# Layer 3's attention: sums of normalized tokens with channels on partitions, Wv applied after the sums

## The chip, the cores and the metric

One core of a Trainium2 chip runs the whole program: four layers over one image of 256 channels and 64 x 64 positions, that is 4096 tokens of 256 channels, all in fp32. The metric is the device time of one execution in microseconds. The engines are TensorE (PE, with its weight loads shown apart as PEld), VectorE (DVE), ScalarE (ACT), GpSimd (POOL) and SyncE (SP, which here issues transfers). Each works through its own queue in order and waits for others by semaphores.

## The reference, cut to the attention of layer 3

The layer norm of the tokens enters a plain attention of one head with 256 channels. Everything around it (two convolution-like layers, another attention, two mixtures of experts) is not touched.

```python
def _ln_t(v, eps=1e-5):
    m = jnp.mean(v, axis=-1, keepdims=True)
    s = jnp.var(v, axis=-1, keepdims=True)
    return (v - m) / jnp.sqrt(s + eps)

def _L3_attn_ref(x, Wq, bq, Wk, bk, Wv, bv):
    Q = jnp.einsum('bsd,de->bse', x, Wq) + bq
    K = jnp.einsum('bsd,de->bse', x, Wk) + bk
    V = jnp.einsum('bsd,de->bse', x, Wv) + bv
    scale = 1.0 / jnp.sqrt(jnp.asarray(Q.shape[-1], dtype=jnp.float32))
    scores = jnp.einsum('bqd,bkd->bqk', Q, K) * scale
    weights = jax.nn.softmax(scores, axis=-1)
    return jnp.einsum('bqk,bkd->bqd', weights, V)

t = t + _L3_attn_ref(_ln_t(t), Wq, bq, Wk, bk, Wv, bv)
t = t + _L3_ffn_ref(_ln_t(t), ...)
```

Since the weights of a query sum to 1, the bias bv can be added to the tokens once, and Wv can be applied before or after the weighted sum over keys: sum(w n) Wv = sum(w (n Wv)).

## The kernel before

The tokens `t` stay in SBUF as 32 tiles of 128 tokens (NT = 32), grouped in 8 blocks of 4 tiles (NBLK, TPB; NB = 512 tokens). Constants: P = 128, C = 256.

The work around the change is `attn3`. It runs in these stages.

1. *The expert layer of layer 2* (`experts`, L1879) writes its rows to `ys` in device memory.
2. *Preparation* (L1884 to L1895), over 8 blocks of 4 tiles. `combine` loads two rows per token from `ys` (one transfer through SP's queue, one through ACT's) and adds both to `t` (L1820, VectorE). `layer_norm` takes mean and variance (L195, L196), the root on ACT (L199), and writes `n` by ACT (L206). `to_channels` transposes it into `nT`, which has channels on partitions (TensorE L217, copies out of PSUM by ACT L220 and VectorE L222). Then Wv is applied to every tile, two tiles to a PSUM bank (L1894, two accumulating matmuls per tile), and ACT copies the result into `v` (L1895), which has 257 columns per tile: the last is 1.0, so that the same matmul that sums the values also sums the exponentials.
3. *The attention loop* (L1925 to L1964), over nine blocks of queries: seven of 4 tiles and two of 2 (`sizes`). For each block it steps over all 32 tiles of keys. A step has `scores(j)`: two matmuls of the key tile with the block's queries into one bank of `s` (three buffers), and an exponential on ACT into `e` (four buffers, L1940). And `values(j)`: for each of the block's query tiles one matmul with a 128x128 piece of `e` as the loaded weights and `v[:, j, :]` streamed past, into that tile's own accumulator `o{i}` (L1945). The scores of step j+1 stand ahead of the values of step j on TensorE. At the end of a block VectorE takes the reciprocal of column 257 and updates the tokens (L1958, L1959).
4. *Between the steps* stand the next block's queries (`queries`, L1916 to L1918, at the step j = 28) and, in portions at j = 3, 7, 11, and so on, the router of the block before (`route`, L1587 to L1645): layer norm, transposes, router matmul, the choice of two experts by small operations of VectorE, and eight indirect transfers issued by POOL. Their PSUM tiles come from `bank()`. PSUM has 8 banks: four for `o`, three for `s`, one (`q`) for queries and router. In the two half blocks two of the `o` banks are lent to `bank()`.
5. After the last block its router portion runs alone, then `tile_table`, then layer 3's expert layer.

Additions that do not depend on the attention also stand in this code: `t += bv3` per block (L1931) and a reduction of `nT` for a guard value (L1933). The order on each queue is settled when the kernel is compiled, by a scheduler that may move independent instructions past each other; on the compiled queue of VectorE the additions and reductions just named stand in the preparation.

Of the kernel before, what the change touches and what calls it, by code (L numbers as in the profile page):

```python
# [10 lines left out]
F32 = mybir.dt.float32  # L11
# [3 lines left out]
ALU = mybir.AluOpType  # L15
# [4 lines left out]
P = 128  # L20
C = 256
HW = 64
N = HW * HW
NT = N // P
NB = 512
NBLK = N // NB
TPB = NB // P
# [51 lines left out]
def bc(ap, axis, n):  # L79

    ap = ap.unsqueeze(axis)
    shape = list(ap.shape)
    shape[axis] = n
    return ap.to_broadcast(shape)


class Net:
# [1766 lines left out]
    def attn3(self, t, S):  # L1854

        nc, tc, w = self.nc, self.tc, self.w

        sizes = [TPB] * (NBLK - 1) + [TPB // 2] * 2  # L1860
        with tc.tile_pool(name="a3", bufs=1) as pool:
            nT = pool.tile([P, 2, N], F32, tag="nT", name="a3_nT")
            v = pool.tile([P, NT, C + 1], F32, tag="v", name="a3_v")
            nc.gpsimd.memset(v[:, :, C : C + 1], 1.0)

            big = pool.tile([P, 2, 2, len(sizes)], F32, tag="big", name="a3_big")
            nc.gpsimd.memset(big, 0.0)
            wqk = pool.tile([P, 2, C], F32, tag="wqk", name="a3_wqk")
            bqk = pool.tile([P, 2], F32, tag="bqk", name="a3_bqk")
            with tc.tile_pool(name="a3m_ps", bufs=1, space=PSUM) as ps:  # L1870
                wT = w["w_qkT3"]
                for m in range(2):
                    p = ps.tile([P, C], F32, tag=f"w{m}", name="a3_w_ps")
                    self.mm(p, [(wT[:, kt, m * P : (m + 1) * P], wT[:, kt, C:]) for kt in range(2)])
                    nc.vector.tensor_copy(wqk[:, m, :], p)
                    p = ps.tile([P, 1], F32, tag=f"b{m}", name="a3_b_ps")
                    self.mm(p, [(wT[:, kt, C + m * P : C + (m + 1) * P], self.par("bq3", kt)) for kt in range(2)])
                    nc.vector.tensor_copy(bqk[:, m : m + 1], p)
            self.experts(S)  # L1879
            with (  # L1880
                tc.tile_pool(name="a3n", bufs=2) as wp,
                tc.tile_pool(name="a3n_ps", bufs=2, space=PSUM) as ps,
            ):
                for b in range(NBLK):  # L1884
                    tiles = slice(b * TPB, (b + 1) * TPB)
                    self.combine(b, t, wp)
                    n = wp.tile([P, TPB, C], F32, tag="n", name="a3_n")
                    self.layer_norm(wp, t[:, tiles, :], n, 1e-5, on_act=True)
                    self.to_channels(ps, "tr", n, nT[:, :, b * NB : (b + 1) * NB])
                    for i in range(0, TPB, 2):  # L1890
                        p = ps.tile([P, 2, C], F32, tag="v", name="a3_v_ps")
                        for j in range(2):
                            at = (b * TPB + i + j) * P
                            self.mm(p[:, j], [(nT[:, kt, at : at + P], w["w_v3"][:, kt, :]) for kt in range(2)])  # L1894
                        nc.scalar.copy(v[:, b * TPB + i : b * TPB + i + 2, :C], p)  # L1895
            with (
                tc.tile_pool(name="a3w", bufs=2) as wp,
                tc.tile_pool(name="a3_ps", bufs=1, space=PSUM) as ps,
            ):
                banks = ["q"]  # L1900

                def bank():
                    banks.append(banks.pop(0))
                    return ps.tile([P, NB], F32, tag=banks[-1], name="a3_q_ps")

                def route(t0, T):
                    rn = wp.tile([P, TPB, CX], F32, tag="rn", name="f_n")
                    rT = wp.tile([P, 2, NB], F32, tag="rT", name="f_nT")
                    return self.route(t0, T, t, S, wp, rn[:, :T], rT[:, :, : T * P], bank)

                def queries(b, t0):
                    T = sizes[b]
                    qT = wp.tile([P, 2, NB], F32, tag="qT", name="a3_qT")[:, :, : T * P]
                    for m in range(2):
                        p = bank()[:, : T * P]
                        self.mm(p, [(wqk[:, kt, m * P : (m + 1) * P], nT[:, kt, t0 * P : (t0 + T) * P]) for kt in range(2)])  # L1916
                        nc.scalar.activation(qT[:, m, :], p, AF.Identity, bias=bqk[:, m : m + 1])
                    nc.vector.tensor_reduce(big[:, 0, :, b : b + 1], qT, AX.X, ALU.max, apply_absolute_value=True)  # L1918
                    return qT

                steps = iter(())
                S["L"] = 3
                qT = queries(0, 0)
                t0 = 0
                for b, T in enumerate(sizes):  # L1925
                    o = [ps.tile([P, NB], F32, tag=f"o{i}", name="a3_o_ps") for i in range(T)]
                    if T < TPB:
                        banks[:] = ["q", "o2", "o3"]

                    part = t[:, t0 : t0 + T, :]  # L1930
                    nc.vector.tensor_tensor(part, part, bc(self.row("bv3"), 1, T), ALU.add)  # L1931
                    if b < NBLK:
                        nc.vector.tensor_reduce(big[:, 1, :, b : b + 1], nT[:, :, b * NB : (b + 1) * NB], AX.X, ALU.max,  # L1933
                                                apply_absolute_value=True)

                    def scores(j):
                        p = ps.tile([P, NB], F32, tag="s", name="a3_s_ps", bufs=3)[:, : T * P]
                        self.mm(p, [(nT[:, m, j * P : (j + 1) * P], qT[:, m, :]) for m in range(2)])
                        e = wp.tile([P, NB], F32, tag="e", name="a3_e", bufs=4)[:, : T * P]
                        nc.scalar.activation(e, p, AF.Exp, scale=1.0 / 16.0)  # L1940
                        return e

                    def values(j, e):
                        for i in range(T):
                            nc.tensor.matmul(o[i][:, : C + 1], e[:, i * P : (i + 1) * P], v[:, j, :], start=(j == 0), stop=(j == NT - 1))  # L1945

                    e = scores(0)
                    for j in range(NT):
                        nxt = scores(j + 1) if j + 1 < NT else None
                        values(j, e)  # L1950
                        e = nxt
                        if j % 4 == 3:
                            next(steps, None)
                        if j == NT - 4 and b + 1 < len(sizes):
                            qT_next = queries(b + 1, t0 + T)
                    for i in range(T):
                        r = wp.tile([P, 1], F32, tag="r", name="a3_r", bufs=4)
                        nc.vector.reciprocal(r, o[i][:, C : C + 1])  # L1958
                        nc.vector.scalar_tensor_tensor(t[:, t0 + i, :], o[i][:, :C], r, t[:, t0 + i, :], ALU.mult, ALU.add)  # L1959
                    qT = qT_next  # L1960
                    for _ in steps:
                        pass
                    steps = route(t0, T)
                    t0 += T  # L1964
                for _ in steps:
                    pass
                self.tile_table(S, wp, bank)

                top = wp.tile([P, 2, 2], F32, tag="top", name="a3_top")
                nc.vector.tensor_reduce(top, big, AX.X, ALU.max)  # L1970
                nc.vector.tensor_tensor(top[:, 0], top[:, 0], top[:, 1], ALU.mult)
                nc.vector.tensor_reduce(self.flags[:, 2:3], top[:, 0], AX.X, ALU.add)
# [235 lines left out]
```

## Time and profile before

| what | us |
|---|---|
| three runs: median (lowest to highest) | 4101.22 (4100.05 to 4104.15) |
| the profiled execution: time, span | 4099.97, 4098.3 |
| preparation: first combine addition to first query matmul | 2502.96 to 2561.22 |
| attention loop: first score matmul to last token update | 2565.86 to 3499.73 |
| one full block of the loop, from one query reduction (L1918) to the next | 2673.21 to 2790.34: 117.13 |
| layer 3's experts: from the first expert transpose (L1743) | 3521.04 |

All times inside the program are counted from the start of the span. Over the span TensorE is busy 87%, VectorE 42%, ACT 31%, GpSimd 35%. These are averages over stages with different limits; what a change in one stage is worth has to be read in that stage. The end of a matmul in the profile is modelled and groups overlap by some 0.2 to 0.4 us, so that distances between starts are to be used, not lengths. An fp32 matmul shows as two rows, each with its own weight load.

### The profile page before, as it was taken

The numbers are of one execution on the slowest core, as the hardware profiler recorded it, in microseconds if no ns is written. First come the engines' busy times: TensorE is split into PE (matmuls) and PEld (weight loads), VectorE is DVE, ScalarE is ACT, GpSimd is POOL, SyncE is SP. The second block draws the span as 40 slices with busy tenths as digits, with TensorE's granted clock in tenths as the row PEclk, the third lists the DMA queues.
The fourth block names the chain that finished last, engine by engine and source line by source line (L and its number), as shares of the span: only waits on it lengthen the run. The fifth ranks groups of instructions, "written<-read, shape, count | busy, mean of one in ns | idle before, by whom it ended". The sixth has DMA issues, their size and how long they took to land.

```text
span 4098.3 us, 57080 instructions
## 1 busy us (share of the span) xinstructions
PE 3563.3 (87%) x21872; PEld 2338.6 (57%) x21872; DVE 1738.9 (42%) x4404; ACT 1267.3 (31%) x2588; POOL 1445.4 (35%) x1376
## 2 busy tenths in 40 slices
PE   7879999999977767656678797999999999799997
PEld 4423433333335656544456575666666668688886
DVE  6876656565653554556566557011011101211111
ACT  4424343434423535311112234122222212233331
POOL 1258898888952243433334341000000001111110
PEclk9989999999998978878778798999999999899999
DMA  1003414210023111110001484000000000455554
GB/s 52 2 26 109 126 57 136 58 39 33 26 94 109 51 44 49 44 30 0 1 11 43 137 259 145 0 10 1 11 11 11 11 11 14 167 193 192 191 190 174
DMA packets 137792, 294.09 MB, mean 72 GB/s; under 512 B 14817, under 2 KB 72802, under 8 KB 128290
## 3 DMA queue, kind: packets, MB, share of 16 engines
q1 hardware_dynamic: 113138, 234.80, 17.7%
q0 software_dynamic: 13056, 35.93, 2.3%
q10 hardware_dynamic: 11312, 19.55, 1.4%
q8 instruction: 178, 2.92, 0.3%
q14 instruction: 108, 0.88, 0.1%
HBM read 202.53 MB, written 87.70 MB: 71 GB/s over the span
## 4 chain that ended last, share of the span: by engine, by line
PE 35%; issue 11%; DVE 5%; POOL 3%; DMA 2%; ACT 1%; SPq 0%; ACTq 0%; POOLq 0%; DVEq 0%
PE a_o_ps L1945 11%; PE a_s_ps L144 11%; PE f_h_ps L144 2%; PE a_qkv_ps L144 2%; PE f_y_ps L144 2%; POOL ys L1782 2%; DMA ys<-f_y,f_at 1%; PE a_q_ps L144 1%; DVE a_sm L1309 1%; PE tr_ps L217 1%; DMA f_g<-ys 1%; PE a_o_ps L144 1%; PE a_u_ps L144 1%; PE a_c_ps L1334 1%; POOL a_tmp L1165 0%
## 5 line engine op out<-in xcount | busy, mean ns | idle before, releaser
L565 POOL TENSOR_TENSOR l_sm<-l_sc,mask 128x512 f32<-128x512 f32 (+3 forms) x624 | 769.9, 1268 | 119.5 <-ACT l_sc L555 117.4
L559 DVE TENSOR_TENSOR l_sm<-l_s,mask 128x256 f32<-128x256 f32 (+3 forms) x1248 | 492.2, 447 | 302.7 <-PE l_s L549 292.9
L555 ACT COPY l_sc<-l_s 128x384 f32<-128x384 f32 (+3 forms) x896 | 367.5, 461 | 558.9 <-PE l_s L549 537.1
L1945 PE MATMUL a_o_ps<-a_v,a_e 128*128 128x257 f32 x2048 | 489.2, 380 | 0.0
L144 PE MATMUL a_s_ps<-a_qT,a_nT 128*128 128x512 f32 (+1 forms) x1152 | 487.8, 546 | 0.0
L1945 PEld LDWEIGHTS a_o_ps<-a_v,a_e 128*128 128x128 f32 x2048 | 388.9, 190 | 147.0 <-issue 103.8
L549 PE MATMUL l_s<-l_q,l_k 32*128 32x384 f32 (+2 forms) x3584 | 423.8, 514 | 7.1 <-ACT l_sc L555 4.1
L1641 POOL DMA_INDIRECT xs<-f_n,f_to x64 | 62.4, 975 | 883.6 <-DVE f_to L1638 840.9
L1940 ACT ACTIVATE a_e<-a_s_ps 128x512 f32<-128x512 f32 (+1 forms) x288 | 158.0, 549 | 687.3 <-PE a_s_ps L144 687.2
L144 PE MATMUL f_h_ps<-f_xT,f_w 128*128 128x256 f32 x1440 | 344.1, 387 | 15.2 <-ACT f_h L1755 5.5
L1782 POOL DMA_INDIRECT ys<-f_y,f_at x144 | 139.6, 970 | 571.3 <-ACT f_y L1781 545.4
L144 PE MATMUL f_y_ps<-f_w,f_h 128*128 128x256 f32 x1440 | 328.1, 379 | 0.0
L144 PEld LDWEIGHTS f_h_ps<-f_xT,f_w 128*128 128x128 f32 x1440 | 264.8, 191 | 83.7 <-ACT f_h L1755 31.5
L854 PE MATMUL l_acc_ps<-ident,l_pr 128*128 128x128 f32 x1600 | 208.9, 291 | 117.8 <-DVE l_pr L850 114.1
L549 PEld LDWEIGHTS l_s<-l_q,l_k 32*128 32x128 f32 x3584 | 164.6, 183 | 240.6 <-issue 123.2
L144 PEld LDWEIGHTS a_s_ps<-a_qT,a_nT 128*128 128x128 f32 x1152 | 216.3, 190 | 129.9 <-issue 112.9
L144 PEld LDWEIGHTS f_y_ps<-f_w,f_h 128*128 128x128 f32 x1440 | 268.2, 190 | 33.7
L854 PEld LDWEIGHTS l_acc_ps<-ident,l_pr 128*128 128x128 f32 x1600 | 193.8, 151 | 132.7 <-DVE l_pr L850 126.4
L850 DVE TENSOR_TENSOR l_pr<-l_vk,l_w_ps 128x1280 f32<-128x1280 f32 x128 | 182.1, 1480 | 91.0 <-ACT l_w_ps L839 79.8
L1755 ACT ACTIVATE f_h<-f_h_ps,f_w 128x256 f32<-128x256 f32 x360 | 163.7, 468 | 131.9 <-PE f_h_ps L144 131.9
L592 PE MATMUL l_a_ps<-l_sm,l_v 128*32 128x512 f32 (+3 forms) x1408 | 179.0, 530 | 1.6 <-POOL l_sm L565 1.5
L592 PE MATMUL l_b_ps<-l_sm,l_v 128*32 128x256 f32 (+2 forms) x2176 | 172.4, 376 | 0.5 <-POOL l_sm L565 0.5
(441 smaller groups left out, 4357.6 us busy)
## 6 DMA issues: line engine op xcount, KB each, us to landing
f_w<-in_f_w SPq DMA_DIRECT2D x36, 1152.0 KB
f_w<-in_f_w SPq DMA_DIRECT2D x36, 1028.0 KB
xs<-zero SPq DMA_DIRECT2D x8, 4160.0 KB
l_vk<-vt SPq DMA_DIRECT2D x180, 128.0 KB
f_x<-xs SPq DMA_DIRECT2D x72, 260.0 KB
f_w<-in_f_w SPq DMA_DIRECT2D x36, 384.0 KB
l_rcp<-l_recd SPq DMA_DIRECT2D x48, 256.0 KB
f_w<-in_f_w SPq DMA_DIRECT2D x36, 257.0 KB
```

The lines of the kernel that those rows point to most:

```text
L144: self.nc.tensor.matmul(out, lhsT, rhs, start=(i == 0), stop=(i == len(pairs) - 1))
L549: nc.tensor.matmul(s[pair, j], k[hp, key * P : (key + 1) * P], qs[hp], start=True, stop=True)
L555: nc.scalar.copy(sc[:, j], s[1, j])
L559: nc.vector.tensor_tensor(sms[0][:, j, at : at + t * wide].rearrange("p (t n) -> p t n", n=wide), part[:, which, :], mask, ALU.mult)
L565: nc.gpsimd.tensor_tensor(sms[1][:, :, at : at + t * wide].rearrange("p j (t n) -> p j t n", n=wide), part[:, :, which, :], bc(mask, 1, 2) ...
L592: nc.tensor.matmul(out, v[:, key, hp], sms[pair][:, j, base + lo * wide : base + hi * wide], start=not seen[nm], stop=(left[nm] == 0 and h ...
L850: nc.vector.tensor_tensor(pr, vk, bc(wps[:, j, dy], 3, D), ALU.mult)
L854: nc.tensor.matmul(acc[:, m, j, :], pf[:, dx, m * P : (m + 1) * P], self.ident, is_transpose=True, start=(j == 0 and dy == 0 and dx == 0 a ...
L1755: nc.scalar.activation(h[:, m, :], q, AF.Gelu, bias=w1[:, 2 * hidden + m : 2 * hidden + m + 1])
L1782: nc.gpsimd.indirect_dma_start(out=self.ys_parts[(i % 4) * NI + k], in_=y[:, k, :], in_offset=None, out_offset=bass.IndirectOffsetOnAxis(a ...
L1940: nc.scalar.activation(e, p, AF.Exp, scale=1.0 / 16.0)
L1945: nc.tensor.matmul(o[i][:, : C + 1], e[:, i * P : (i + 1) * P], v[:, j, :], start=(j == 0), stop=(j == NT - 1))
```

## The change

Wv leaves the preparation. The normalized tokens `n` are kept whole (32 tiles of 256 columns) in the room that `v` had. In a step of the loop `values(j)` no longer loads pieces of `e`: it loads the two 128-channel halves of `n[:, j]` and streams `e` (512 query columns, 256 in half blocks) past them, into two accumulators `z0`, `z1` with channels on partitions. The exponentials are summed by VectorE into `tot` (a copy for j = 0, an addition for each later step). When a block ends, ACT copies `z0` and VectorE `z1` into `zs`. The rest of the block's end, `go()`, is issued in the next block after its step j = 1: per tile a matmul of `tot` with a column of ones, one reciprocal, two matmuls of `zs` with Wv per tile (into banks of the tag `s`), and the token updates; it returns the block's router generator, whose portions follow at j = 3, 7, and so on as before. Since the accumulators take two banks instead of four, `bank()` rotates over three. After the last block `go()` runs by itself ahead of the router.

```diff
-            v = pool.tile([P, NT, C + 1], F32, tag="v", name="a3_v")
-            nc.gpsimd.memset(v[:, :, C : C + 1], 1.0)
+            n = pool.tile([P, NT, C], F32, tag="n", name="a3_n")
...
                     self.combine(b, t, wp)
-                    n = wp.tile([P, TPB, C], F32, tag="n", name="a3_n")
-                    self.layer_norm(wp, t[:, tiles, :], n, 1e-5, on_act=True)
-                    self.to_channels(ps, "tr", n, nT[:, :, b * NB : (b + 1) * NB])
-                    for i in range(0, TPB, 2):
-                        p = ps.tile([P, 2, C], F32, tag="v", name="a3_v_ps")
-                        for j in range(2):
-                            at = (b * TPB + i + j) * P
-                            self.mm(p[:, j], [(nT[:, kt, at : at + P], w["w_v3"][:, kt, :]) for kt in range(2)])
-                        nc.scalar.copy(v[:, b * TPB + i : b * TPB + i + 2, :C], p)
+                    self.layer_norm(wp, t[:, tiles, :], n[:, tiles, :], 1e-5, on_act=True)
+                    self.to_channels(ps, "tr", n[:, tiles, :], nT[:, :, b * NB : (b + 1) * NB])
...
-                banks = ["q"]
+                banks = ["q0", "q1", "q2"]
...
+                def finish(t0, T, z, tot):
+
+                    zs = wp.tile([P, 2, NB], F32, tag="zs", name="a3_zs", bufs=1)[:, :, : T * P]
+                    nc.scalar.copy(zs[:, 0], z[0])
+                    nc.vector.tensor_copy(zs[:, 1], z[1])
+
+                    def go():
+                        r_ps = bank()[:, :T]
+                        for i in range(T):
+                            self.mm(r_ps[:, i : i + 1], [(tot[:, i * P : (i + 1) * P], self.ones_col)])
+                        r = wp.tile([P, TPB], F32, tag="r", name="a3_r")[:, :T]
+                        nc.vector.reciprocal(r, r_ps)
+                        for i in range(0, T, 2):
+                            p = ps.tile([P, 2, C], F32, tag="s", name="a3_o_ps", bufs=3)
+                            for j in range(2):
+                                at = slice((i + j) * P, (i + j + 1) * P)
+                                self.mm(p[:, j], [(zs[:, m, at], w["w_v3"][:, m, :]) for m in range(2)])
+                            for j in range(2):
+                                out = t[:, t0 + i + j, :]
+                                nc.vector.scalar_tensor_tensor(out, p[:, j], r[:, i + j : i + j + 1], out, ALU.mult, ALU.add)
+                        return route(t0, T)
+                    return go
...
-                    o = [ps.tile([P, NB], F32, tag=f"o{i}", name="a3_o_ps") for i in range(T)]
-                    if T < TPB:
-                        banks[:] = ["q", "o2", "o3"]
+                    z = [ps.tile([P, NB], F32, tag=f"z{m}", name="a3_z_ps")[:, : T * P] for m in range(2)]
+                    tot = wp.tile([P, NB], F32, tag="tot", name="a3_tot")[:, : T * P]
...
                     def values(j, e):
-                        for i in range(T):
-                            nc.tensor.matmul(o[i][:, : C + 1], e[:, i * P : (i + 1) * P], v[:, j, :], start=(j == 0), stop=(j == NT - 1))
+                        for m in range(2):
+                            nc.tensor.matmul(z[m], n[:, j, m * P : (m + 1) * P], e, start=(j == 0), stop=(j == NT - 1))
+                        if j == 0:
+                            nc.vector.tensor_copy(tot, e)
+                        else:
+                            nc.vector.tensor_tensor(tot, tot, e, ALU.add)
...
-                        if j % 4 == 3:
+                        if j == 1 and left:
+                            steps = left()
+                        if j > 1 and j % 4 == 3:
                             next(steps, None)
...
-                    for i in range(T):
-                        r = wp.tile([P, 1], F32, tag="r", name="a3_r", bufs=4)
-                        nc.vector.reciprocal(r, o[i][:, C : C + 1])
-                        nc.vector.scalar_tensor_tensor(t[:, t0 + i, :], o[i][:, :C], r, t[:, t0 + i, :], ALU.mult, ALU.add)
+                    left = finish(t0, T, z, tot)
                     qT = qT_next
                     for _ in steps:
                         pass
-                    steps = route(t0, T)
                     t0 += T
-                for _ in steps:
+                for _ in left():
                     pass
```

More of the change, by code (lines that the diff above doesn't have):

```diff
@@ L1919, in queries @@
                     return qT
-                steps = iter(())
+                def finish(t0, T, z, tot):
[18 more added lines that the diff above has]
+                    return go
+                steps, left = iter(()), None
                 S["L"] = 3
```

## The prediction, made before the changed kernel ran

> **What bounds the kernel now.** I read the busy slices of the page first, then the stages around the change, then the order of instructions inside them. Columns of a stage line: its bounds and length in us, busy time and instructions of PE, PEld, DVE, ACT and POOL, granted clock, DMA share, GB/s.
>
> ```profile
> 2502.90:2515.00 12.10, 0.00 (x0) 0.00 (x0) 11.22 (x29) 1.81 (x3) 0.00 (x0) 0.50 0.67 244
> 2515.00:2539.20 24.20, 21.75 (x93) 16.70 (x94) 22.39 (x66) 16.26 (x36) 0.00 (x0) 0.83 0.49 174
> 2539.20:2557.50 18.30, 16.21 (x88) 13.62 (x87) 18.24 (x35) 12.34 (x26) 0.32 (x2) 1.00 0.00 0
> 2800.00:2917.00 117.00, 117.00 (x421) 77.31 (x420) 11.57 (x51) 23.79 (x40) 7.96 (x9) 1.00 0.03 10
> ```
>
> The first three lines are the preparation of layer 3's attention, the fourth is one block of its loop. In the preparation VectorE is the full engine (22.39 of 24.20 us, then 18.24 of 18.30); TensorE has gaps. In the loop TensorE is busy for all 117 us at clock 1.00 and VectorE for 11.57. What goes from the first stage into the second therefore leaves a half-hidden place for one where every TensorE row counts.
>
> The order on TensorE inside the loop (start, length, instruction; the length of a group holds a modelled end, so I use differences of starts):
>
> ```profile
> 2746.55 1.88 PE L144 MATMUL a_s_ps<-a_qT,a_nT 128*128 128x512 f32 x4
> 2748.26 1.90 PE L1945 MATMUL a_o_ps<-a_v,a_e 128*128 128x257 f32 x8
> 2749.99 1.88 PE L144 MATMUL a_s_ps<-a_qT,a_nT 128*128 128x512 f32 x4
> 2751.71 1.90 PE L1945 MATMUL a_o_ps<-a_v,a_e 128*128 128x257 f32 x8
> ...
> 3393.95 1.03 PE L144 MATMUL a_s_ps<-a_qT,a_nT 128*128 128x256 f32 x4
> 3394.81 1.03 PE L1945 MATMUL a_o_ps<-a_v,a_e 128*128 128x257 f32 x4
> ```
>
> One fp32 matmul shows as two rows. A step of the loop is 4 rows of 512 columns (1.72 us, 0.430 each) and 8 rows of 257 (1.73 us, 0.216 each): 3.45 us, without a gap. From 257 to 512 columns a row grows by 0.214 us for 255 columns, 0.00084 per column; 257 of these are 0.2155, so hardly 1 ns of a row is a fixed cost. In the two half blocks a row of 256 columns takes the same 0.216 us, a step 1.73.
>
> **The change, part by part**, against the profiled execution (4099.97 us, span 4098.3; the median of the runs is 1.25 above it).
>
> *Loop step.* Before: 4 x 0.430 + 8 x 0.216. After: 4 rows of scores and 4 rows of sums, all of 512 columns, 8 x 0.430 = 3.44 us. The step loses 0.01 us; 7 full blocks x 32 steps give -2.2 us. A half step is 8 rows of about 256 columns before and after: 0.
>
> *Wv moved into the loop.* Each block's finish issues two matmuls per tile, 4 rows of 256 columns. Seven blocks of 4 tiles: 7 x 16 x 0.216 = +24.2; the first half block: 8 x 0.216 = +1.7. The last half block's falls into the tail, below.
>
> *Row sums of the exponentials.* One matmul of one column per tile, 2 rows. No such row exists. Nearest are the router's rows of 8 columns: the step that holds 16 of them lasts 5.23 us between exponentials instead of 3.45, so 0.111 each. The rows after are narrower, but the column of 257 they replace is already counted; bounds 0.05 (a shorter stream) and 0.216 (a full row). I take 0.111, the row it is nearest to: 7 x 8 x 0.111 + 4 x 0.111 = +6.7, bounds +3 and +13.
>
> *Three banks for queries and router.* The second query matmul waited for the copy of the first (the row at 2904.73 began about 0.1 us after its turn, released by the copy; eight places): -0.8. Nothing else in the loop waited for a bank.
>
> *VectorE's sums.* 32 additions of 128x512 per block. The bias addition of that shape (L1931) took 0.68 us: 22 us on an engine that uses 11.57 of 117, so 0 on the path; the cover is VectorE's idle 105 us. The new wait: the exponential of step j+4 takes the buffer of step j and so waits for its addition, some 10 us of slack. Queued on VectorE ahead of additions are the router's operations (about 3.7 us in one run at most) and the layer norm's reciprocal, which waits for a Sqrt between two table loads on ACT (2.8 us, L199 and L1940). They come after the fourth exponential, while TensorE is in the Wv rows, and neither eats the slack. A gain is excluded, as VectorE holds nothing up there now; the loss is the first rival. Copying the sums out at a block's end (ACT and VectorE, some 0.7 us each by the 128x512 copies) hides behind the 8 score rows that follow, 3.4 us.
>
> Loop: -2.2 + 24.2 + 1.7 + 6.7 - 0.8 = **+29.6 us**.
>
> *Tail.*
>
> ```profile
> 3498.20 0.17 DVE L1958 RECIPROCAL a_r<-a_o_ps 128x1 f32<-128x1 f32 x1 [18.73 <-PE a_o_ps L1945]
> 3499.26 0.47 DVE L1959 SCALAR_TENSOR_TENSOR t<-a_o_ps,a_r,t 128x256 f32<-128x256 f32 x1
> ```
>
> The last token update ends at 3499.73 with nothing behind it but the router's chain. After the change the second half of the sums is complete at about 3498.65, its copy takes 0.42 (a 128x256 copy from PSUM, L1605), then 8 rows of 0.216 and 0.2 to be seen, then a 0.47 update: 3501.6. **+1.9 us.**
>
> *Preparation.*
>
> ```profile
> 2555.64 1.22 DVE L1933 TENSOR_REDUCE a_big<-a_nT 128x2 f32<-128x1024 f32 x1
> 2556.77 0.68 DVE L222 COPY a_nT<-tr_ps 128x512 f32<-128x512 f32 x1
> 2556.83 3.72 PE L144 MATMUL a_v_ps<-w_v,a_nT 128*128 128x256 f32 x16 [0.29 <-ACT a_nT L220]
> ...
> 2560.59 0.58 ACT L1895 COPY a_v<-a_v_ps 128x512 f32<-128x512 f32 x1 [0.71 <-PE a_v_ps L144]
> 2561.22 1.98 PE L144 MATMUL a_q_ps<-a_nT,a_wqk 128*128 128x512 f32 x4 [0.68 <-ACT a_v L1895]
> ```
>
> What goes: 128 rows on TensorE (27 us at speed) and 16 ACT copies (9.3 us). VectorE loses nothing, and VectorE bounds the stage. So two things are won. The end, from the last nT copy (2557.45) to the first query (2561.22): 3.8 us less 0.2 for a wakeup, 3.6. And the order: the compiled queues show twelve additions and reductions of 1.2 us (L1931, L1933), which nobody waits for, between the last combine addition and the last nT copy; eight in the changed kernel. 4 x 1.2 = 4.8. I leave VectorE's other 1.8 us of idle time as it is. Sum -8.4, bounds -3.6 (the order wins nothing, as the copy then waits for the normalisation on ACT) and -15 (22 us from the last addition at 2539.2 to the query shrink to a bare chain of 7: stats 1.9, Sqrt and small ones 1, normalisation 2.1, transposes and copy 2). Then the second query matmul no longer waits for the first's copy (2564.03 instead of 2562.94): -1.1.
>
> *The clock at the loop's start.* With TensorE nearly idle in the preparation, the loop begins slow. The rows that show this:
>
> ```profile
> 3521.00:3526.00 5.00, 1.09 (x4) 0.71 (x4) 1.88 (x10) 0.00 (x0) 0.00 (x0) 0.50 0.96 350
> 3526.00:3530.00 4.00, 3.76 (x9) 3.07 (x10) 0.36 (x2) 1.55 (x2) 0.00 (x0) 0.50 0.98 387
> 3530.00:3534.00 4.00, 4.00 (x19) 3.47 (x19) 0.92 (x8) 2.33 (x6) 0.00 (x0) 0.97 1.02 419
> ```
>
> After an idle stretch TensorE got 9 rows done in 4 us, then 19. Four us at half speed cost **+2.0**; without a fall of the clock 0. The Trainium skill ("TensorE: Matmul & The Clock Gate", section "Why this matters for your kernels") asks for 4 us of continuous work and no idle gaps over about 3 us, which would make the same slow start; in the preparation after the change each block leaves such gaps around its transposes.
>
> A rule also argues for the change: the Trainium skill ("Perfetto Trace Analysis", section "Matmuls") says larger matmuls are more efficient when possible. By "TensorE: Matmul & The Clock Gate", section "Back-to-back issue gap", each pays about 2.5 ns on top of its columns; as an estimate, 4 rows fewer per step would save 0.010 us by it, the same -2.2 us as by the rows: right in sign, too small.
>
> **Sum:** 29.6 + 1.9 - 8.4 - 1.1 + 2.0 = +24.0; 4099.97 + 24.0 = **4124 us**. Bounds of the unknown terms: low 24.0 - 3.7 (sums) - 6.6 (preparation) - 2.0 (clock) = +11.7; high 24.0 + 6.3 + 4.8 = +35.
>
> **Rivals.**
> 1. *VectorE's sums hold up the exponentials.* For: a strict queue, with a wait for ACT's Sqrt and its two table loads (2 x 1.28 us) ahead of additions, most of all in half blocks, whose step is 1.73 us. Against: 33 us of work in a block of 121. Price: one table pair and Sqrt, 2.8 us, exposed in each of nine blocks, 25 us: 4149, half of it 4136.
> 2. *Faster: value rows are slowed by their weight loads.* A load of e (L1945, 190 ns) fills nearly all of a 216 ns row, and the sums halve these loads. If 25 ns of each such row were load, a step would fall by 8 x 0.025 = 0.20 and the full blocks by 224 x 0.20 = 45 us, 43 more than counted: 4081. It decides from about 0.15 per step. Against: half steps, whose score rows have the same loads, and the column slope above; a load wait of 25 ns would show as a fixed part, and that is 1 ns.
> 3. *No difference.* The preparation gives its full 15, the sums cost 3, the clock does not fall, and the loop saves 0.02 a step rather than 0.01: 24.0 - 6.6 - 3.7 - 2.0 - 2.2 = +9.5, 4109, the edge of what counts as same.
>
> **How the numbers follow.** Forecast 0.74, rival 1 0.12, rival 2 0.07, rival 3 0.07. A measurement of this kernel tells 0.2% (8.2 us) from no change, so from 4109.4 it is slower: forecast and rival 1, 0.86; same 0.07; faster 0.07. The range takes in both bounds and the lighter half of rival 1: 4110 to 4138; rivals 2 and 3 and the heavy half of 1 stay out.
>
> **What would show it.** Right: a full block of 121 us instead of 117.1, steps of 3.44 with TensorE still at 117 of 117; a group of 16 rows into the output tile of about 3.5 us early in each block from the second on; no a_v_ps; the first query near 2553 with a clock of 0.5; the last token update near 3524 instead of 3499.7. Wrong: idle time on TensorE ahead of the sums, released by the exponentials and these by the additions (rival 1); a step clearly below 3.4 us (rival 2); a query start before 2547 (rival 3).

## The result, and the profile after

| | us |
|---|---|
| kernel before, median of 4 runs (lowest to highest) | 4100.78 (4100.05 to 4104.15) |
| changed kernel, median of 4 runs | 4123.40 (4121.44 to 4128.35) |
| ratio, 95% interval | 1.0055, 1.0038 to 1.0073 |
| profiled execution of the changed kernel: time, span | 4124.94, 4123.1 |

The change costs 22.6 us (0.55%). The ratio's interval makes that 16 to 30 us; 4124.0 was forecast.

The stages of the changed kernel, with the columns of the stage lines in the prediction. The first line is the last 29 us of the preparation, up to the first query; the second is one block of the loop.

```profile
2527.00:2556.05 29.05, 13.05 (x48) 7.35 (x49) 28.69 (x71) 16.27 (x35) 0.32 (x2) 0.50 0.20 75
2666.93:2787.69 120.76, 120.76 (x318) 57.11 (x317) 34.01 (x82) 24.52 (x40) 8.47 (x9) 1.00 0.03 9
```

In the loop TensorE is still busy for every microsecond, at clock 1.00; a block now lasts 120.76 us instead of 117.13. VectorE's busy time in it has tripled, from 11.57 to 34.01, and that is hidden. In the preparation TensorE is busy for less than half of the time and gets half its clock, while VectorE is full.

TensorE early in a block, from the timeline (start, length, instruction, count):

```profile
2679.74 1.88 PE L144 MATMUL a_s_ps<-a_qT,a_nT 128*128 128x512 f32 x4
2681.46 1.88 PE L1959 MATMUL a_z_ps<-a_e,a_n 128*128 128x512 f32 x4
2683.18 0.95 PE L144 MATMUL a_q_ps<-one,a_tot 128*128 128x1 f32 x8
2683.99 3.70 PE L144 MATMUL a_o_ps<-w_v,a_zs 128*128 128x256 f32 x16
2687.52 1.88 PE L144 MATMUL a_s_ps<-a_qT,a_nT 128*128 128x512 f32 x4
```

From start to start, a step is 2683.18 - 2679.74 = 3.44 us (eight rows of 0.43), the eight rows of the sums take 0.81 (0.101 each) and the sixteen rows of Wv 3.53 (0.22 each). No bracket of idle time stands behind any line: TensorE goes from one group to the next.

The end of the preparation and of the loop:

```profile
2552.60 2.16 PE L217 MATMUL tr_ps<-ident,a_n 128*128 128x128 f32 x8 [2.04 <-ACT a_n L206]
2554.10 1.21 DVE L1947 TENSOR_REDUCE a_big<-a_nT 128x2 f32<-128x1024 f32 x1
2555.23 0.68 DVE L222 COPY a_nT<-tr_ps 128x512 f32<-128x512 f32 x1
2556.05 5.22 PE L144 MATMUL a_q_ps<-a_nT,a_wqk 128*128 128x512 f32 x8 [1.29 <-DVE a_nT L222]
...
3519.36 1.89 PE L1959 MATMUL a_z_ps<-a_e,a_n 128*128 128x256 f32 x8
3521.45 1.97 PE L144 MATMUL a_o_ps<-w_v,a_zs 128*128 128x256 f32 x8
3523.46 0.88 DVE L1932 SCALAR_TENSOR_TENSOR t<-a_o_ps,a_r,t 128x256 f32<-128x256 f32 x2 [1.67 <-PE a_o_ps L144]
```

The last copy of nT stands behind a reduction for which nobody waits, and it releases the first query. The last token update ends at 3523.46 + 0.88 = 3524.34.

To compare runs I count from the end of the last matmul of layer 2's experts, because the stages before that move from run to run. Ahead of the preparation the two programs differ only in the tile `v` or `n` and in the write of ones into `v` (0.16 us on POOL at 2322.25, for which nobody waits), and yet that matmul ended at 2491.72 us in the profile of before and at 2496.25 in that of after; in a later profile of the unaltered changed kernel, on another chip, it ended at 2517.57. From there:

| us after the last expert matmul | before | after | difference |
|---|---|---|---|
| first query matmul | 69.50 | 59.80 | -9.70 |
| first score matmul | 74.14 | 64.86 | -9.28 |
| last token update | 1008.01 | 1028.09 | +20.08 |
| from there to the end of the span | 598.57 | 598.76 | +0.19 |

So the change itself costs 20.1 us in this pair of profiles; 4.5 of the 24.8 us between the two spans came before it and, as that stage moves by itself, are not counted as part of it.

### The profile page after: what moved, and what is told of

Its sections match the earlier page's. It is cut to its first block, busy times and chain, and to the rows that moved or that the text cites. A ratio compares the mean times of both kernels' runs of the same rounds, so it can differ in the third digit from the quotient of the medians.

```text
span 4123.1 us, 55899 instructions
## 1 busy us (share of the span) xinstructions
PE 3567.6 (87%) x21040; PEld 2177.5 (53%) x21040; DVE 1921.4 (47%) x4678; ACT 1264.8 (31%) x2581; POOL 1449.8 (35%) x1375
## 4 chain that ended last, share of the span: by engine, by line
PE 35%; issue 11%; DVE 5%; DMA 3%; POOL 2%; ACT 1%; SPq 0%; ACTq 0%; DVEq 0%; POOLq 0%
PE a_s_ps L144 11%; PE a_z_ps L1959 11%; PE f_h_ps L144 2%; PE a_qkv_ps L144 2%; PE f_y_ps L144 2%; POOL ys L1782 2%; DMA ys<-f_y,f_at 1%; PE a_o_ps L144 1%; PE a_q_ps L144 1%; PE tr_ps L217 1%; DMA f_g<-ys 1%; DVE a_sm L1309 1%; PE a_u_ps L144 1%; PE a_c_ps L1334 1%; POOL a_tmp L1165 0%
## 5 line engine op out<-in xcount | busy, mean ns | idle before, releaser
L1959 PE MATMUL a_z_ps<-a_e,a_n 128*128 128x512 f32 (+1 forms) x1152 | 484.9, 545 | 0.0
L1963 DVE TENSOR_TENSOR a_tot<-a_tot,a_e 128x512 f32<-128x512 f32 (+1 forms) x279 | 176.4, 632 | 561.9 <-ACT a_e L1954 561.5
L1954 ACT ACTIVATE a_e<-a_s_ps 128x512 f32<-128x512 f32 (+1 forms) x288 | 158.1, 550 | 694.1 <-PE a_s_ps L144 694.0
L1959 PEld LDWEIGHTS a_z_ps<-a_e,a_n 128*128 128x128 f32 x1152 | 218.7, 190 | 220.8 <-issue 214.3
```

What stands on the lines that cost most here:

```text
L1959: nc.tensor.matmul(z[m], n[:, j, m * P : (m + 1) * P], e, start=(j == 0), stop=(j == NT - 1))
L1963: nc.vector.tensor_tensor(tot, tot, e, ALU.add)
```

## The experiments

Ten kernels ran, in three comparisons on three chips, each beside the kernel before, which took 4099.27, 4134.12 and 4130.28 us there. Read their ratios and the distances inside their traces, not their absolute times.

**Wv's matmuls twice** (first comparison):

```diff
-                                self.mm(p[:, j], [(zs[:, m, at], w["w_v3"][:, m, :]) for m in range(2)])
+                                for _ in range(2):
+                                    self.mm(p[:, j], [(zs[:, m, at], w["w_v3"][:, m, :]) for m in range(2)])
```

> The changed kernel with each of the matmuls with Wv at a block's end issued twice into the same PSUM bank, the second overwriting the first: 64 matmuls, 128 rows of 256 columns more, and nothing else. Theory (in the loop TensorE sets the time, so a Wv row costs what it lasts, 0.22 us): 7 x 16 x 0.22 = +24.6 in the full blocks' finishes, +1.8 and about +1.8 for the two half blocks, +28 us, 4151 us; a full block of 124.3 us instead of 120.8. Rival (part of the rows hides behind waits for the exponentials or the sums): less than +20, and idle time on TensorE that shrinks.

Measured: 4151.27 us (4148.94 to 4157.70), ratio 1.0126 (1.0111 to 1.0142). The timeline shows the group doubled and the next scores as much later, and a block of 124.21 us instead of 120.76:

```profile
2680.71 7.15 PE L144 MATMUL a_o_ps<-w_v,a_zs 128*128 128x256 f32 x32
2687.70 1.88 PE L144 MATMUL a_s_ps<-a_qT,a_nT 128*128 128x512 f32 x4
```

Sixteen more rows cost 3.45 us (124.21 - 120.76), 0.216 each, to the full. Wv's rows in the loop lie on the path with their whole length.

**VectorE's additions twice**, into a second total that nobody reads:

```diff
+                            nc.vector.tensor_copy(tot2, e)
...
+                            nc.vector.tensor_tensor(tot2, tot2, e, ALU.add)
```

> The changed kernel with every exponential added by VectorE into a second total as well, which nobody reads: 288 more operations, 22 us more VectorE work per full block (34 of 121 us become 56). Theory (VectorE's sums lie under TensorE): 0, within 3 us of the changed kernel's 4123, and the same 120.8 us per block. Rival (sums hold buffers of the exponentials now and then): each hold doubles; if they cost 5 us or more in the changed kernel, at least +5.

Measured: 4123.15 us (4119.35 to 4131.70), ratio 1.0052 (1.0039 to 1.0066). One block in the stage view:

```profile
2671.00:2791.76 120.76, 120.76 (x318) 57.12 (x317) 52.97 (x113) 24.52 (x41) 8.93 (x9) 1.00 0.03 9
```

VectorE works 52.97 us instead of 34.01 and the block is not 0.01 us longer; from the first score to the last update lie 963.22 us, against 963.23. Rival 1 falls. The changed kernel's own groups say it too (busy and mean ns, then idle time ahead and what ended it):

```profile
L1963 DVE TENSOR_TENSOR a_tot<-a_tot,a_e 128x512 f32<-128x512 f32 (+1 forms) x279 | 176.4, 632 | 561.9 <-ACT a_e L1954 561.5
L1954 ACT ACTIVATE a_e<-a_s_ps 128x512 f32<-128x512 f32 (+1 forms) x288 | 158.1, 550 | 694.1 <-PE a_s_ps L144 694.0
```

The exponentials waited 694.1 us in all, 694.0 of it for scores. The additions wait for the exponentials, and the other way round the profile shows next to nothing.

**Wv back in the preparation**, everything else as changed. At a block's end the sums are only transposed back:

```diff
+                    for i in range(0, TPB, 2):
...
+                            self.mm(p[:, j], [(nT[:, kt, at : at + P], w["w_v3"][:, kt, :]) for kt in range(2)])
+                        nc.scalar.copy(v[:, b * TPB + i : b * TPB + i + 2, :], p)
...
-                                self.mm(p[:, j], [(zs[:, m, at], w["w_v3"][:, m, :]) for m in range(2)])
+                                for m in range(2):
+                                    nc.tensor.transpose(p[:, j, m * P : (m + 1) * P], zs[:, m, at], self.ident)
```

> The changed loop, but with Wv applied in the preparation as in the kernel before (128 rows on TensorE, 16 copies on ACT) and the values' sums, which then have channels on partitions, turned back at a block's end by two transposes per tile instead of the matmuls with Wv. Theory (the loss is Wv's new place): preparation as long as before, +9.7 - 0.4 against the changed kernel; a finish of 8 transposes of 0.11 us instead of 16 rows of 0.22, so -2.6 in each of seven blocks and -1.3 in each half block, -21. Sum about -12, 4111 us, which leaves +10 against the kernel before: sums by matmul 6.5, transposes 7, steps -4.5, tail 1.5. Rival (the orientation or VectorE's sums cost, not Wv's place): stays at 4120 or more.

Measured: 4107.39 us (4106.69 to 4115.39), ratio 1.0025 (1.0016 to 1.0034). A block takes 118.13 us. Eight transposes stand where sixteen rows stood:

```profile
2693.31 1.07 PE L1937 MATMUL a_o_ps<-ident,a_zs 128*128 128x128 f32 x8
2694.22 1.88 PE L144 MATMUL a_s_ps<-a_qT,a_nT 128*128 128x512 f32 x4
```

They take 0.91 us from start to start, against Wv's 3.53: 2.62 less, and the block is 120.76 - 118.13 = 2.63 shorter. The first query starts at 69.50 us after the last expert matmul, to the hundredth as before the change. So all of the preparation's gain belongs to Wv's absence from it, and without moving Wv the new loop still costs 0.25%.

**The bias additions and the guard's reductions moved out of the preparation**, into the blocks of the changed kernel:

```diff
-                    part = t[:, t0 : t0 + T, :]
-                    nc.vector.tensor_tensor(part, part, bc(self.row("bv3"), 1, T), ALU.add)
                     if b < NBLK:
+                        nc.vector.tensor_copy(big[:, 1, :, b : b + 1], big[:, 0, :, b : b + 1])
...
+                        part = t[:, t0 : t0 + T, :]
+                        nc.vector.tensor_tensor(part, part, bc(self.row("bv3"), 1, T), ALU.add)
                         return route(t0, T)
```

The added copy only makes the reduction wait for the block's queries; the reduction overwrites it.

> The changed kernel with the bias additions moved behind each block's token update and the guard reductions of nT held back until the block's queries exist, so that neither stands on VectorE's queue in the preparation. Theory (VectorE with these fillers bounds the changed preparation: 13.4 us from the last combine addition to the first query, 9.7 of them fillers): the stretch shrinks to about 8, -5 to -6 us, +0.7 in the tail: 4118 us. Rival (the chain normalisation on ACT, transposes, copies bounds it): 0 to -2 us.

Measured: 4118.67 us (4113.10 to 4126.12), ratio 1.0047 (1.0033 to 1.0061). The intervals overlap; the trace is sharper: the first query starts at 56.60 us instead of 59.80, the last update ends at 1025.21 instead of 1028.09. The expected 5 us were 3.2 in the stage.

**Unread Wv rows in the preparation of the changed kernel** (second comparison), for blocks 0 to 6, without the copies to `v`:

```diff
+                    for i in range(0, TPB if b < NBLK - 1 else 0, 2):
+                        p = ps.tile([P, 2, C], F32, tag="v", name="a3_v_ps")
+                        for j in range(2):
+                            at = (b * TPB + i + j) * P
+                            self.mm(p[:, j], [(nT[:, kt, at : at + P], w["w_v3"][:, kt, :]) for kt in range(2)])
```

> The changed kernel with 16 more Wv matmuls (rows of 128x256) after the transposes of each of the preparation's blocks 0 to 6; nobody reads their results. They keep TensorE busy where it idled and leave VectorE's and ScalarE's work as it is. Theory (the cold clock is a small cost of its own): the transposes of a block go back from 2.16 to about 1.04 us and the first query from 5.22 to about 3.7, so the first score comes 2 to 3 us sooner and the time is 4121 (4119 to 4123). Rival (the clock does not matter at the loop's start, or the added rows delay the transposes): 4123 to 4126.

Measured: 4159.23 us (4145.47 to 4162.48), ratio 1.0054 (1.0036 to 1.0073): nothing gained. Theory and rival each had half of it. The clock was 1.00, a block's transposes took 1.04 us instead of 2.16 and the way from first query to first score 3.51 us instead of 5.06. But the first query came at 64.50 us instead of 59.80. VectorE's order could be the reason, or the rows themselves; the next run separates the two.

**The same rows with the late additions**, that is the last two edits together:

> The unread Wv rows in the preparation and, with them, the bias additions and guard reductions moved out of it, so that the compiled order has nothing to put before VectorE's last copies of nT. It is to be read beside the run with the late additions alone (from the last expert matmul's end to the first score 61.84 us, to the last token update 1025.21 us). Theory (the unread rows cost 4.8 us only through VectorE's order, and a warm clock is worth about 1.6 us at the first query and some 1 us at the last transposes): first score at 58.5 to 60.5 us, last update at 1022 to 1024 us. Rival (the rows themselves hold up the transposes): first score at 62 us or later.

Measured: 4151.88 us (4149.77 to 4159.69), ratio 1.0058 (1.0044 to 1.0072); first query at 63.80 us, first score at 67.30, last update at 1031.60. The theory fell, the rival held. The start of the first query in the four kernels:

| us after the last expert matmul | additions in the preparation | moved out |
|---|---|---|
| unread Wv rows | 64.50 | 63.80 |
| no Wv rows | 59.80 | 56.60 |

From the second block's transposes to the first query, moving the additions out takes 11.3 us of VectorE's work away with the rows there (30.09 to 18.82) and brings 0.7 us; without the rows it takes 8.4 away (30.76 to 22.38) and brings 3.2. The lines of that stretch, of this kernel, then of the one with late additions alone:

```profile
2553.84:2585.09 31.25, 28.64 (x154) 24.06 (x152) 18.82 (x60) 15.94 (x34) 0.32 (x2) 1.00 0.19 68
```

```profile
2521.28:2549.06 27.78, 15.22 (x56) 8.62 (x57) 22.38 (x67) 18.31 (x39) 0.32 (x2) 0.50 0.30 108
```

With rows TensorE is busy 28.64 of 31.25 us and VectorE 18.82. TensorE sets the pace, since a block's transposes are queued behind the Wv rows of the block before:

```profile
2578.34 1.04 PE L217 MATMUL tr_ps<-ident,a_n 128*128 128x128 f32 x8
2579.62 3.72 PE L144 MATMUL a_v_ps<-w_v,a_nT 128*128 128x256 f32 x16 [0.24 <-ACT a_nT L220]
2583.17 1.04 PE L217 MATMUL tr_ps<-ident,a_n 128*128 128x128 f32 x8
```

Rows, transposes and a short wait for the copy of nT: 4.83 us per block (2583.17 - 2578.34).

**The changed kernel once more**, in the same comparison:

> The changed kernel once more, unaltered, beside the run with late additions and unread rows and the kernel before in the same comparison. Expected: 1.0055 of the kernel before (1.0038 to 1.0073), 1028 us from the last expert matmul's end to the last token update, and 2 to 6 us above the run with late additions and unread rows.

Measured: 4149.05 us (4147.72 to 4152.99), ratio 1.0049 (1.0035 to 1.0063), as expected; last update at 1030.17 us. It was not slower than the run before it, so the last part of the expectation missed. Its first query and score lay 6.34 us apart instead of 5.06. Between two profiles of one kernel the first query thus moved by 0.05 us and the last update by 2.1; differences of that size in the last update say nothing.

**The preparation interleaved with the first block** (second comparison). If TensorE's idle time in the preparation is what made Wv cheap there, it can be used in another way. `prep(b)` is the body of the preparation's loop, in the same pools as the attention, with `bank()` rotating over one query bank and the two of the transposes:

```diff
-                for b in range(NBLK):
+                def prep(b):
...
+                prep(0)
                 qT = queries(0, 0)
+                prep(1)
...
                         e = nxt
+                        if b == 0 and j % 4 == 0 and j // 4 + 2 < NBLK:
+                            prep(j // 4 + 2)
```

> The changed kernel with the preparation of block b+2 written between the steps of the first attention block (every fourth step), in the same pools; the same work, only its order is other. Theory (TensorE's work costs its length only while TensorE sets the end; in the preparation VectorE does): the first query starts some 32 us sooner (near 2524 instead of 2556 on the changed kernel's time line), seven groups of transposes of 1.04 us come into the loop, so 4123.4 - 32 + 7 = 4098, with up to 10 us of stalls 4098 to 4108, and no block after the first differs from 120.76 us. Rival (in the first block VectorE's combinations or ScalarE's changes between square root and exponential hold up the steps): what is saved is lost again, 4117 or more.

Measured: 4125.73 us (4112.81 to 4136.42) where the kernel before took 4134.12, ratio 0.9978 (0.9965 to 0.9992): by its ratio faster than both kernels. The first query starts at 25.56 us instead of 59.80, the last update ends at 1001.40 instead of 1028.09 (after) or 1008.01 (before). The first block in the stage view, and one block's transposes in it:

```profile
2538.99:2657.42 118.43, 118.33 (x311) 54.98 (x312) 63.75 (x126) 50.61 (x84) 0.00 (x0) 0.98 0.09 28
```

```profile
2552.53 1.04 PE L217 MATMUL tr_ps<-ident,a_n 128*128 128x128 f32 x8
2553.41 1.02 PE L144 MATMUL a_s_ps<-a_qT,a_nT 128*128 128x512 f32 x2
```

TensorE is busy 118.33 of 118.43 us, with 63.75 us of VectorE's work beside it. A block's transposes cost 0.88 us (2553.41 - 2552.53), and none of the feared waits came: 34.2 us sooner, less seven times 0.88 and 2.0 for a slow first query, leaves 26.0 of the 26.7 us gained, where the theory had 25.

**The interleaved kernel with the late additions:**

> The interleaved kernel with the bias additions and the guard's reductions moved out of the preparation, as in the run that did only this (which gained 4.7 us). Theory: with TensorE setting the end through the preparation VectorE's fillers cost nothing there, so it is within 1.5 us of the interleaved kernel. Rival (VectorE still sets the end of the interleaved preparation): 3 to 5 us better than that.

Measured: 4119.14 us (4113.72 to 4130.99), ratio 0.9965 (0.9947 to 0.9982), last update at 1000.83 us: 0.6 us from the interleaved kernel in the trace, with overlapping intervals. Where TensorE sets the end, VectorE's additions are worth nothing more.

**The interleaved kernel with Wv in the preparation**, the edits of the third experiment on top:

> The interleaved kernel with Wv applied in the preparation and transposes at the ends of the blocks, as in the run with Wv back in the preparation (which was 16 us faster than the changed kernel). Theory: the place of Wv is worth 16 us only because TensorE idles in the preparation; interleaved it must pay 8 x 3.5 = 28 us of Wv rows there and saves 8 x 2.63 = 21 us at the blocks' ends, so it is some 7 us slower than the interleaved kernel (3 to 10). Rival (TensorE still idles enough in the interleaved preparation to take the rows for nothing): 10 to 21 us faster than it.

Measured: 4134.33 us (4116.32 to 4139.85), ratio 0.9994 (0.9980 to 1.0008); last update at 1007.36 us, 6.0 later than with Wv at the blocks' ends, within the 3 to 10 expected. Without interleaving Wv in the preparation was 12.7 us better by the same distance (1015.43 against 1028.09). With the changed loop, the sign of moving Wv depends on whether TensorE idles in the preparation; the old loop was not interleaved in any run. In the stage view, from the first Wv row to the end of the first block, it does not:

```profile
2551.16:2696.28 145.12, 145.12 (x439) 79.54 (x440) 64.25 (x126) 54.84 (x96) 0.00 (x0) 0.99 0.07 23
```

## Why the prediction was right, and which terms were off

The forecast, Wv's rows paid in full in the loop against a smaller gain in the preparation, is what happened, and the time is 0.6 us from it. The terms against the trace:

| term of the sum | predicted | measured |
|---|---|---|
| Wv's rows in the loop | +25.9 | +25.9 at the 0.216 of the doubled rows (7 x 3.45, and 8 x 0.216) |
| sums of the exponentials | +6.7 | +6.7 (the other 0.89 of a full block's 4.34, or 0.111 a row) |
| loop step | -2.2 | -3.8 (224 x 0.017) |
| half steps | 0 | -0.3 (64 x 0.004: 1.730 to 1.726) |
| three banks | -0.8 | -1.1 (six times 0.18; the half blocks' queries did not wait) |
| tail | +1.9 | +1.95 (3.03 to 4.98 from the start of the last sums over keys to the last update) |
| preparation | -8.4 | -9.7 |
| second query without its wait | -1.1 | -1.1 (4.64 to 3.54 in the run with Wv back in the preparation) |
| slow clock | +2.0 | +1.5 (3.54 to 5.06) |

The measured terms add up to about +20. Wv's rows and the sums are safe only together: by the starts of the groups they are 3.53 and 0.81 of the 4.34. In the prediction the parts of the tail add up to 3501.47, so +1.7 and not +1.9.

The loop from first score to last update went from 933.87 to 963.23 us, +29.4 where loop and tail were put at +31.5. Everything together was +20.1 in the trace against +24.0. That the total lies so near 4124.0 is partly luck: the medians differ by 22.6 us, and the interval cannot tell 20 from 24; and the last update came at 3524.34, as forecast, only because the stage ahead of the change ended 4.5 us later.

- *Loop step.* Mis-sized. TensorE's values 13 steps apart, in the first block of before and of after:

```profile
2572.93 1.90 PE L1945 MATMUL a_o_ps<-a_v,a_e 128*128 128x257 f32 x8
2617.78 1.90 PE L1945 MATMUL a_o_ps<-a_v,a_e 128*128 128x257 f32 x8
```

```profile
2568.16 1.88 PE L1959 MATMUL a_z_ps<-a_e,a_n 128*128 128x512 f32 x4
2612.79 1.88 PE L1959 MATMUL a_z_ps<-a_e,a_n 128*128 128x512 f32 x4
```

44.85 us against 44.63: steps of 3.450 and 3.433, 0.017 less and not 0.01. "Hardly 1 ns of a row is a fixed cost" was worked out from three-digit means; over 13 steps a row of 512 columns is 0.4292 us and one of 257 is 0.2167, so the fixed part is about 2.5 ns, the value of the prediction's other estimate. Four rows and eight columns fewer make up the 0.017. It is nearer to rival 3's 0.02 than to the forecast's 0.01.
- *Sums.* The nearest row, 0.111, held.
- *VectorE's sums* cost nothing, even doubled.
- *Preparation.* The size was nearly right, and half of the cause was wrong. The end came as forecast: from the start of the last copy of nT to the first query it was 4.45 us and is 0.82, 3.6 less. The other 6.1 were put at 4.8 for a different order of VectorE's additions, because "VectorE bounds the stage". That does not hold. The order changed as read from the queues (eight long additions and reductions instead of twelve stand between the last combination and the last copy), but the experiments show that with the rows in place TensorE's own sequence sets the pace, and the additions fill VectorE's waits. The rows of blocks 0 to 6 account for 4.7 of the 6.1 (first query at 64.50 and 59.80). The other 1.4 are gone already with the unread rows, where the last copy of nT starts at 63.67 instead of 65.05; that kernel also lacks the copies to `v`, but no run separates their part. VectorE sets the pace only once the rows are gone, and then for 3.2 us. The line "18.24 of 18.30" in the profile of before was read as a bound; TensorE's 16.21 of 18.30 beside it, with gaps of 0.29 to 0.85 that all wait for copies, was the engine to follow. In that profile too, a block's transposes start where the rows of the block before end:

```profile
2550.40 1.04 PE L217 MATMUL tr_ps<-ident,a_n 128*128 128x128 f32 x8
2551.94 3.72 PE L144 MATMUL a_v_ps<-w_v,a_nT 128*128 128x256 f32 x16 [0.51 <-ACT a_nT L220]
2555.50 1.04 PE L217 MATMUL tr_ps<-ident,a_n 128*128 128x128 f32 x8
```

- *Clock.* Mis-sized, and not one number: between first query and first score lie 3.50 to 3.54 us where the preparation kept TensorE busy, and 5.06 to 6.58 in four runs of kernels whose preparation is that of the changed one: 1.5 to 3.1 us. The gaps around the transposes were shorter than the "over about 3 us" that the prediction gave them: by TensorE's idle times 2.0 to 3.7 us between blocks, one of them over 3, with the granted clock at 0.50 from 2515.00 to 2556.05.
- *Rival 2*, value rows held up by weight loads: a step of 3.43 us, not 3.25. It falls. Rival 1 fell by the doubled additions, rival 3 by the measured difference, though its value for the step was the better one.

## What to carry to other kernels

Before moving work between stages, ask on both sides what its engine would otherwise do: taking Wv's 128 rows and their copies out of a preparation where TensorE has gaps saved 9.7 us, 120 of these rows cost 26 us in a loop where it has none (the other eight are in the tail), and when the preparation was laid over the loop the better place changed. An engine that is full in a profile need not set the pace; it may be filling waits with work that nobody needs yet. Take that filler out and see whether the end moves. And a stage in which TensorE idles can be overlapped with the next one's matmuls: here that was worth more (last update at 1001.40 us) than filling it with Wv (1015.43).

## What the runs showed of the hardware that was not expected

- The slow start after a sparse stage varies without any change of code. With the changed kernel's preparation, first query to first score took 5.06, 6.15, 6.34 and 6.58 us; the query rows stood 0.85 us apart until the granted clock came back, then 0.43. The Trainium skill ("TensorE: Matmul & The Clock Gate", section "What's actually happening") says that the activity window runs freely, so that the count of cold matmuls differs from run to run and is not to be fitted; the four runs vary as it says. The roughly 3.4 us that it gives for the cold stretch was exceeded: in the run with 6.58 us the rows stayed 0.85 apart for over 5 us.
- A matmul row that streams one column takes 0.101 us from start to start, or 0.111 if the Wv rows behind it are put at their 0.216: about half of a row of 256 columns. Rows of 257 and of 512 columns grow in proportion to their columns, with about 2.5 ns on top; one of a single column has a floor far above its share.
